# A sequential edge-removal pass beside four graph layers: the nearest removal handed over in SBUF instead of through DRAM

## The chip, the cores and the metric

The kernel runs on one core of one Trainium2 chip. The metric is the device time of one execution in microseconds (us). The time before is 6935.3 us, the median of three runs (6930.78 to 6940.25). One more execution was recorded by the hardware profiler; its span is 6932.5 us. The engines are named as in the profile: PE (matrix products), PEld (its weight loads), DVE (vector), ACT (scalar), POOL (GpSimd) and SP (SyncE, which here only issues DMAs).

## The reference, cut to what matters

Sixteen graphs of 1024 nodes with 128 features pass four layers with a residual and a layer norm after each. The first three (masked attention, a max over neighbours, a sum over neighbours with an MLP) use the adjacency as given. The fourth uses an adjacency from which edges have been removed first, row by row, each removal also changing later rows:

```python
def step(carry, n):
    row = carry[n]
    num = sum(row)
    sf = where(num > 10, (num + 1) // 2, 1)
    rank = cumsum(row)
    rm = row & (rank % sf == 0)          # only where the node counts and num > 1
    carry = carry.at[n].set(row & ~rm)
    carry = carry.at[:, n].set(carry[:, n] & ~rm)     # the symmetric column
    return carry
# for n = 0 .. 1023, in this order; then three rounds of
#   agg = (adj_d @ x) / deg;  out = normalised(agg @ Wr + x @ Wx + b);  h = batchnorm(relu(out))
```

The important point is the last line of the step: an edge removed in row n at position m must also be missing when row m is reached. A removal in one row has to be handed on, transposed, to all rows that come later.

## The kernel before

**Two stages.** `layers_012` computes the first three layers for one graph after another. The removal pass (`dilation`) depends only on the adjacency, so it runs beside them, for all 16 graphs at once. After that, the fourth layer runs alone (`edges`, `sage`, `convolve`).

**Slots.** The first stage is a loop over 1376 slots (86 for each of 16 graphs). In each half of a slot PE looks up a table (`look_up`, L769, into the PSUM tile `pg`, two buffers) and DVE takes a maximum of it (`best`, L821, 128x1024 elements). Everything else is put between these: generators yield the engine and cost of their next piece, and `advance` emits a piece where the planned room of its engine allows it. The instruction order of PE, ACT, DVE and POOL is the order in which this Python code emits them (`manual_schedule`). SP is not in that list: the order of the DMAs on its queue comes from the framework's scheduler. SP issues them one after another.

**Blocks of the removal pass.** The 1024 rows are cut into K = 32 blocks of R = 32 rows. A block of all 16 graphs lies on 128 partitions as 4 groups of 32 rows, with Q = 4 graphs side by side in the free dimension: `E` is [128, 4, 1024] of bytes. Two blocks go by for one graph of the slots, so that even blocks contain the start of a graph (`attend`, `scores` and the tables of the next graph begin there) and odd blocks don't. Block k runs through these steps, each due at a slot fixed by the numbers that `dilation` yields:

1. L578 and L579: edges that the block before removed are taken out of `E`; they come from SBUF as `next_T`. `spread` (L581) opens the block: it sums counts per row with a small matmul (L588).
2. 31 rows on POOL (L602 to L618). Each row is a chain of ten tiny POOL instructions on 16 partitions that decides what is removed inside the 32x32 square, and writes `hit`. One row follows from the one before.
3. Between the rows, one turn of `work` per row on DVE: first `remove` of block k-1 (`behind`), then `prepare` of block k+1.
4. `hit` goes to DRAM (L623) and comes back in another layout as `hit_p` (L626); DVE takes it out of `E` (L630 to L634) and works out each row's step and rank. The removal in the next block's columns is transposed at once into `next_T` (L668).

**`remove(k)`** ranks the edges of the whole row block (two scans, L553, per graph of a partition), marks the removed ones in `gone` (L559, two buffers), stores them to `removed` (L561, for the fourth layer), transposes those two and more blocks ahead into `last_T` (L564, one buffer, [128, 4, blocks after, 32]), and stores that to `removed_T` in DRAM (L565). It takes 16 turns.

**`prepare(k)`** builds `V`, the ranks inside the square, sends it through DRAM to 16 partitions (L521, L522), then reads everything that blocks 0 to k-2 removed from `removed_T` into `gone_T` (L526, one DMA for each q, one buffer), passes five empty turns, and takes it out of `E` (L533, one instruction for each q, the remaining edges summed into `counts[:, 0]`). ACT sums the columns to the right (L538).

The order of work around the change is thus: `removed_T` writes of block k-1 and `gone_T` reads for block k+1 both fall into the rows of block k, on the queue of SP, on which `hit`, `hit_p`, `above` and `V` stand too.

Of the kernel before, what the change touches and what calls it, by code (L numbers as in the profile page):

```python
# [29 lines left out]
F32 = mybir.dt.float32  # L30
F32R = mybir.dt.float32r
BF = mybir.dt.bfloat16
# [3 lines left out]
ALU = mybir.AluOpType  # L36
# [3 lines left out]
B, N, D, H2 = 16, 1024, 128, 256  # L40
P = 128
# [5 lines left out]
NP = -(-N // PS)  # L47
TG = 12
R, G = 32, 4
K, Q = N // R, B // G  # L50
# [21 lines left out]
def tile_graph_layers(ctx: ExitStack, tc, a, out):  # L72
    nc = tc.nc
# [93 lines left out]
    for b in range(B):  # L167
        q, g = divmod(b, G)
        nc.gpsimd.dma_start(out=half_rows[g * R:(g + 1) * R, :, q],
                            in_=a["nodemask"][b].rearrange("(k r) -> r k", r=R))  # L170
    nc.vector.tensor_scalar(half_rows, half_rows, 0.5, None, op0=ALU.mult)

    of_graph = consts.tile([P, G], F32, name="of_graph")
# [17 lines left out]
    removed_T = dram.tile([K, P, Q, N], BF, name="removed_T")  # L191
# [44 lines left out]
    def layers_012():  # L236
# [6 lines left out]
        dil = right.enter_context(tc.tile_pool(name="dil", bufs=1, side="right"))  # L243
# [237 lines left out]
        def dilation():  # L481
            adj_q = adj.rearrange("(q g) n m -> g n q m", g=G)
            axis = mybir.AxisListType.X
            hit = dil.tile([B, R, R], BF, name="hit")
            nc.gpsimd.memset(hit, 0.0)

            def load(k):
                own = slice(k * R, (k + 1) * R)
                E = dil.tile([P, Q, N], U8, name="E", bufs=3)
                for g in range(G):  # L490
                    nc.gpsimd.dma_start(out=E[g * R:(g + 1) * R], in_=adj_q[g, own])


                counts = dil.tile([P, 5, Q], F32, name="counts", bufs=2)
                nc.gpsimd.memset(counts, 0.0)
                V = dil.tile([B, R, R], BF, name="V", bufs=2)
                return E, V, counts

            def prepare(k, E, V, counts):
                own = slice(k * R, (k + 1) * R)  # L500
                square = dil.tile([P, Q, R], BF, name="square")
                nc.vector.tensor_copy(square, E[:, :, own])
                square_T = dil.tile([P, Q, R], BF, name="square_T")
                nc.vector.transpose(square_T.rearrange("p q m -> p (q m)"), square.rearrange("p q m -> p (q m)"))
                upper = dil.tile([P, Q, R], BF, name="upper")
                nc.vector.tensor_mul(upper, square, above)
                nc.vector.tensor_reduce(counts[:, 3, :], square, axis=axis, op=ALU.add)
                yield 1.3
                U = dil.tile([P, Q, R], BF, name="U")
                nc.vector.tensor_tensor_scan(U.rearrange("p q m -> p (q m)"), running.rearrange("p q m -> p (q m)"),  # L510
                                             upper.rearrange("p q m -> p (q m)"), 0.0, op0=ALU.mult, op1=ALU.add)
                nc.vector.tensor_copy(counts[:, 4, :], U[:, :, R - 1])
                nc.vector.tensor_sub(counts[:, 3, :], counts[:, 3, :], counts[:, 4, :])
                nc.vector.tensor_mul(upper, upper, square_T)
                far = dil.tile([P, Q, R], F32, name="far")
                nc.vector.scalar_tensor_tensor(far, U, FAR, upper, op0=ALU.add, op1=ALU.mult)
                Vp = dil.tile([P, Q, R], BF, name="Vp")
                nc.vector.tensor_scalar(Vp, far, -1.0, FAR, op0=ALU.mult, op1=ALU.add)
                Vd = dram.tile([B, R, R], BF, name=f"above{k}")
                for g in range(G):  # L520
                    nc.sync.dma_start(out=Vd.rearrange("(q g) n m -> g n q m", g=G)[g], in_=Vp[g * R:(g + 1) * R])  # L521
                nc.sync.dma_start(out=V, in_=Vd)  # L522
                if k > 1:
                    gone_T = dil.tile([P, Q, N], BF, name="gone_T")
                    for q in range(Q):
                        nc.sync.dma_start(out=gone_T[:, q, :(k - 1) * R],  # L526
                                          in_=removed_T[k, :, q, :(k - 1) * R])
                yield 2.0
                for _ in range(5):
                    yield 0  # L530
                for q in range(Q):
                    if k > 1:
                        nc.vector.scalar_tensor_tensor(  # L533
                            E[:, q, :(k - 1) * R], E[:, q, :(k - 1) * R], 1.0, gone_T[:, q, :(k - 1) * R],
                            op0=ALU.mult, op1=ALU.is_gt, accum_out=counts[:, 0, q:q + 1])
                    if k < K - 1:
                        junk = dil.tile([P, N], U8, name="junk")
                        nc.scalar.activation(junk[:, :N - (k + 1) * R], E[:, q, (k + 1) * R:], AF.Copy,  # L538
                                             accum_out=counts[:, 1, q:q + 1])
                    yield 0.6  # L540

            def remove(k, E, centre, scale, width):

                own = slice(k * R, (k + 1) * R)
                after = K - 2 - k
                if after > 0:
                    last_T = dil.tile([P, Q, after, R], BF, name="last_T")
                ranks = [None] * Q
                for q in range(Q + 1):
                    if q < Q:  # L550
                        rank = ranks[q] = dil.tile([P, N], F32, name="rank", bufs=2)
                        for h, s in enumerate(halves):
                            nc.vector.tensor_tensor_scan(rank[:, s], E[:, q, s], E[:, q, s],  # L553
                                                         rank[:, 511:512] if h else 0.0, op0=ALU.add, op1=ALU.max)
                            yield 1.3
                        nc.scalar.activation(rank, rank, AF.Abs, bias=centre[:, q:q + 1], scale=scale[:, q:q + 1])
                    if q:
                        gone = dil.tile([P, N], BF, name="gone", bufs=2)
                        nc.vector.scalar_tensor_tensor(gone, ranks[q - 1], width[:, q - 1:q], E[:, q - 1, :],  # L559
                                                       op0=ALU.is_equal, op1=ALU.mult)  # L560
                        nc.sync.dma_start(out=removed[k, :, q - 1, :], in_=gone)  # L561
                        yield 1.3
                        if after > 0:
                            nc.vector.transpose(last_T[:, q - 1].rearrange("p k r -> p (k r)"), gone[:, (k + 2) * R:])  # L564
                            nc.sync.dma_start(out=removed_T[k + 2:, :, q - 1, own].rearrange("k p r -> p k r"),  # L565
                                              in_=last_T[:, q - 1])
                            yield 0.8

            this, next_T = load(0), None
# [1 line left out]
                pass  # L571
            behind = iter(())
            for k in range(K):
                E, V, counts = this
                own = slice(k * R, (k + 1) * R)
                if k:
                    prev = slice((k - 1) * R, k * R)
                    nc.vector.tensor_tensor(E[:, :, prev], E[:, :, prev], next_T, op=ALU.is_gt)  # L578
                    nc.vector.tensor_reduce(counts[:, 2, :], E[:, :, prev], axis=axis, op=ALU.add)  # L579
                spread = dil.tile([P, 5, Q, G], F32, name="spread")  # L580
                nc.vector.tensor_mul(spread, counts.unsqueeze(3).to_broadcast([P, 5, Q, G]),  # L581
                                     of_graph.unsqueeze(1).unsqueeze(1).to_broadcast([P, 5, Q, G]))
                yield 0, 0.9, True
                p = shared("pc")
                own_bank = hold()
                for c, slots in enumerate(((0, 2, 3), (1, 4))):
                    for i in slots:
                        nc.tensor.matmul(p[:B, c * R:(c + 1) * R], spread[:, i].rearrange("p q g -> p (q g)"), of_row,  # L588
                                         start=(i == slots[0]), stop=(i == slots[-1]))
# [6 lines left out]
                work = [behind]  # L596
# [3 lines left out]
                work = (cost for part in work for cost in part)  # L600
                gp = nc.gpsimd
                for n in range(R - 1):  # L602
# [12 lines left out]
                    gp.tensor_scalar(last[:, n + 1:], V[:, n, n + 1:], to, None, op0=ALU.is_le)  # L615
                    gp.tensor_add(hit[:, n, n + 1:], hit[:, n, n + 1:], last[:, n + 1:])
                    gp.tensor_sub(low[:, n + 1:], low[:, n + 1:], hit[:, n, n + 1:])
                    yield 1.05, next(work, 0), False  # L618
                for cost in work:
                    yield 0.5, cost, False  # L620

# [3 lines left out]
                for g in range(G):  # L625
                    nc.sync.dma_start(out=hit_p[g * R:(g + 1) * R],  # L626
                                      in_=hit_d.rearrange("(q g) n m -> g n q m", g=G)[g])
                yield (B * NP - 10) / K - 34.55, 0, False
                hit_T = dil.tile([P, Q, R], BF, name="hit_T")
                nc.vector.transpose(hit_T.rearrange("p q m -> p (q m)"), hit_p.rearrange("p q m -> p (q m)"))  # L630
                nc.vector.tensor_tensor(E[:, :, own], E[:, :, own], hit_T, op=ALU.is_gt)
                nc.vector.tensor_reduce(counts[:, 3, :], E[:, :, own], axis=axis, op=ALU.add)
                num = dil.tile([P, Q], F32, name="num")
                nc.vector.tensor_reduce(num, counts[:, 0:4, :].rearrange("p s q -> p q s"), axis=axis, op=ALU.add)  # L634
                yield 0.5, 1.2, False

                half = dil.tile([P, Q], F32, name="half")
                nc.vector.scalar_tensor_tensor(half, num, 0.5, half_rows[:, k, :], op0=ALU.add, op1=ALU.mult)
# [521 lines left out]
```

## Time and profile before

| stretch of the span, us | length | PE busy | DVE busy | ACT busy | POOL busy |
|---|---|---|---|---|---|
| 0 to 136.2: weights, first graph's scores | 136.2 | 77.3 | 33.0 | 48.4 | 28.6 |
| 136.2 to 5560: slots with the removal pass | 5423.8 | 4511.4 | 4652.2 | 3149.4 | 3549.1 |
| 5560 to 6932.5: fourth layer | 1372.5 | 1100.0 | 616.4 | 538.8 | 262.7 |

The first bound of the second stretch is the first `spread` (L581), the last one lies after the last block's `hit_T` (L630). Busy time alone doesn't say what an engine is worth: an engine at 86% may be the one that all others wait for, and its idle time may have one cause or many. The views used below are: the 40 slices of the page; the groups of instructions by line, which give after the second bar the idle time of the engine just before them and what ended it; the waits (who waited for whom, total, times, longest); the time-line of one engine; and busy time by stretch. An "SPq" line is an issue or a wait of SP's queue. The granted clock of PE was 0.887 of full speed over the span.

### The profile page before, as it was taken

To read this page: it belongs to the slowest core of one execution; us is meant where nothing else is said; L and a number is where in the kernel's file an instruction comes from. 1 tells how busy PE (TensorE), PEld (TensorE's weight loads), DVE (VectorE), ACT (ScalarE), POOL (GpSimd) and SP (SyncE) were. 2 spreads that over 40 slices of the span, in tenths; PEclk is the share of its full clock that TensorE was granted. 3 is DMA by queue.
4 is the path that set the end of the run, shared out by engine and by line. 5 is a ranking of instruction groups with operands and counts; after the bars stand their busy time and mean duration, and the time that the engine had idled before them with its cause. 6 is when DMAs were issued, how large, how long until landed. Compare 5 with 4: busy or idle time off the path is not lost. (4 is left out here: it accounts for less than half of the span.)

```text
span 6932.5 us, 85659 instructions
## 1 busy us (share of the span) xinstructions
PE 5688.7 (82%) x27113; PEld 2882.3 (42%) x27242; DVE 5301.6 (76%) x8046; ACT 3736.6 (54%) x6537; POOL 3840.5 (55%) x11285
## 2 busy tenths in 40 slices
PE   6869898989697878888887878787897868787996
PEld 3424344444343434343443434343443335555653
DVE  3979899999797888888887979797898944444453
ACT  4646566666465555555565656565565523333851
POOL 3655767776657575757575757575777611110116
PEclk8979898999798989898988888888898878888998
DMA  5111212121212121212121212121211046554644
GB/s 36 16 21 21 32 24 33 20 32 19 32 20 26 25 27 24 27 24 27 24 29 22 30 21 30 21 30 21 32 20 23 14 74 115 112 112 110 215 140 158
DMA packets 494380, 318.97 MB, mean 46 GB/s; under 512 B 316650, under 2 KB 445668, under 8 KB 489828
## 3 DMA queue, kind: packets, MB, share of 16 engines
q0 software_dynamic: 105648, 84.20, 13.9%
q1 hardware_dynamic: 383600, 228.10, 11.4%
q8 instruction: 213, 3.49, 0.2%
q10 hardware_dynamic: 4676, 1.19, 0.1%
q14 instruction: 243, 1.99, 0.1%
HBM read 413.70 MB, written 118.16 MB: 77 GB/s over the span
## 5 line engine op out<-in xcount | busy, mean ns | idle before, releaser
L821 DVE TENSOR_TENSOR best<-best,pg 128x1024 f32<-128x1024 f32 x2720 | 3230.1, 1210 | 307.9 <-PE pg L769 298.9
L739 ACT ACTIVATE hot<-pm,one_less 128x512 fp32r<-128x512 f32 x2752 | 1884.9, 689 | 1257.8 <-PE pm L738 1246.9
L769 PE MATMUL pg<-hot,high 64*128 64x512 f32 x5504 | 1476.9, 533 | 763.3 <-DVE best L821 694.9
L769 PEld LDWEIGHTS pg<-hot,high 64*128 64x128 f32 x5504 | 546.8, 195 | 1569.5 <-DVE best L821 1076.6
L769 PE MATMUL pg<-hot,low 64*128 64x512 f32 x5504 | 1170.7, 422 | 0.0
L738 PE MATMUL pm<-AT,lit 120*128 120x512 fp8e4 x2752 | 1139.4, 414 | 7.9 <-ACT low L760 1.6
L607 POOL TENSOR_SCALAR sc<-low_counts,half_mask,rest 16x1 f32<-16x1 f32 x992 | 433.0, 436 | 397.6 <-DVE rest L594 304.1
L769 PEld LDWEIGHTS pg<-hot,low 64*128 64x128 f32 x5504 | 571.8, 204 | 0.0
L738 PEld LDWEIGHTS <-lit 120*128 120x128 fp8e4 x2752 | 274.2, 100 | 621.8 <-issue 558.1
L760 ACT CAST low<-pt 128x256 fp32r<-128x256 f32 x688 | 256.0, 372 | 473.6 <-PE pt L758 469.5
L612 POOL TENSOR_SCALAR sc<-sc 16x1 f32<-16x1 f32 x992 | 426.8, 430 | 105.1
L609 POOL TENSOR_SCALAR sc<-sc 16x1 f32<-16x1 f32 x992 | 351.6, 354 | 107.7
L970 POOL TENSOR_TENSOR length<-length,mhalf 128x8 f32<-128x8 f32 x48 | 78.9, 1644 | 571.7 <-DVE length L969 571.7
L615 POOL TENSOR_SCALAR last_rank<-V,sc 16x31 f32<-16x31 bf16 (+30 forms) x992 | 377.2, 380 | 0.0
L614 POOL TENSOR_SCALAR hit<-V,sc 16x31 bf16<-16x31 bf16 (+30 forms) x992 | 375.7, 379 | 0.0
L758 PE MATMUL pt<-high,less 128*128 128x256 f32 x688 | 300.5, 437 | 67.4 <-ACT high L753 60.7
L533 DVE SCALAR_TENSOR_TENSOR E<-E,gone_T 128x32 uint8<-128x32 uint8 (+29 forms) x120 | 80.2, 669 | 325.4 <-DMA gone_T<-removed_T 325.4
L467 DVE TENSOR_TENSOR sub<-sub,q 128x24 f32<-128x24 f32 (+11 forms) x768 | 304.8, 398 | 24.7 <-ACT q L289 10.5
L750 PE MATMUL pt<-ident,sub 128*128 128x128 f32 x1376 | 293.7, 298 | 34.7 <-ACT hot L739 32.1
L610 POOL TENSOR_SCALAR sc<-sc 16x1 f32<-16x1 f32 x992 | 272.4, 275 | 83.3
L927 ACT CAST m<-near 128x1024 fp32r<-128x1024 fp8e4 x256 | 253.4, 1045 | 112.9 <-DVE near L896 59.9
L377 PE MATMUL pav<-v,eT 128*128 128x128 f32 x2048 | 307.3, 296 | 2.0 <-ACT eT L370 2.0
(255 smaller groups left out, 9614.6 us busy)
## 6 DMA issues: line engine op xcount, KB each, us to landing
removed<-gone SPq DMA_DIRECT2D x128, 256.0 KB
An<-in_adj_dram POOLq DMA_DIRECT2D x16, 1024.0 KB, 15.7
E<-in_adj_dram POOLq DMA_DIRECT2D x128, 128.0 KB, 6.7
gone_all<-removed POOLq DMA_DIRECT2D x64, 256.0 KB, 12.0
near<-in_adjT_dram POOLq DMA_DIRECT2D x16, 1024.0 KB, 17.4
h<-x SPq DMA_DIRECT2D x32, 512.0 KB
kept<-near SPq DMA_DIRECT2D x16, 1024.0 KB
share<-share SPq DMA_DIRECT2D x32, 512.0 KB
```

What stands on the lines that cost most here:

```text
L377: nc.tensor.matmul(pav, eT[:, c, :], values[b][:, c, :], start=(c == 0), stop=(c == T - 1))
L467: nc.vector.tensor_max(sub[:, :n_g, n:2 * n], sub[:, :n_g, 0:n], qg[:, 2 * g0:2 * g0 + n_g, k:k + 1].to_broadcast([P, n_g, n]))
L607: gp.tensor_scalar(half, mine, half_mask[:, m], rest[:, n:n + 1], op0=ALU.mult, op1=ALU.add)
L609: gp.tensor_scalar(sf, half, 5.5, sf, op0=ALU.is_gt, op1=ALU.mult)
L612: gp.tensor_scalar(to, at, sf, none, op0=ALU.subtract, op1=ALU.subtract)
L614: gp.tensor_scalar(hit[:, n, n + 1:], V[:, n, n + 1:], at, None, op0=ALU.is_equal)
L615: gp.tensor_scalar(last[:, n + 1:], V[:, n, n + 1:], to, None, op0=ALU.is_le)
L738: nc.tensor.matmul(pm, lit[:, r, :], AT[b * (T + 1) + c][:, halves[h]], start=True, stop=True)
L739: nc.scalar.activation(hots[s][:, halves[h]], pm, AF.Relu, bias=one_less)
L758: nc.tensor.matmul(pt, less, high, start=False, stop=True, skip_group_check=True)
L769: nc.tensor.matmul(pg[:, a], part[rows, at * P:(at + 1) * P], hots[s][rows, halves[h]], start=(k == 0), stop=(k == 1))
L821: nc.vector.tensor_max(own, own, pg)
```

## The change

What block k+1 needs of the removal in block k-1 is already in SBUF when it is prepared: it is the first of the blocks in `last_T`. The change takes it from there, with a comparison and a sum of its own and a sixth slot in `counts`. Only what blocks 0 to k-2 removed then comes through DRAM, and that was written a block earlier; so the read of `gone_T` is moved from the middle of the rows to `load`, which is called ahead of the first row. It is meant to take the trip through DRAM out of the rows in which the removal is made. The five empty turns, which had given that trip time, go, and the rows become due every 1.03 slots instead of 1.05 with the pause after them adjusted, so that a block has the same number of slots.

```diff
+            last_T = None
             def load(k):
...
+                gone_T = None
+                if k > 2:
+                    gone_T = dil.tile([P, Q, N], BF, name="gone_T")
+                    for q in range(Q):
+                        nc.sync.dma_start(out=gone_T[:, q, :(k - 2) * R],
+                                          in_=removed_T[k, :, q, :(k - 2) * R])
...
-                counts = dil.tile([P, 5, Q], F32, name="counts", bufs=2)
+                counts = dil.tile([P, 6, Q], F32, name="counts", bufs=2)
...
-            def prepare(k, E, V, counts):
+            def prepare(k, E, V, gone_T, counts):
...
                 nc.sync.dma_start(out=V, in_=Vd)
+                yield 2.0
                 if k > 1:
-                    gone_T = dil.tile([P, Q, N], BF, name="gone_T")
-                    for q in range(Q):
-                        nc.sync.dma_start(out=gone_T[:, q, :(k - 1) * R],
-                                          in_=removed_T[k, :, q, :(k - 1) * R])
-                yield 2.0
-                for _ in range(5):
-                    yield 0
+                    at = slice((k - 2) * R, (k - 1) * R)
+                    nc.vector.tensor_tensor(E[:, :, at], E[:, :, at], last_T[:, :, 0, :], op=ALU.is_gt)
+                    nc.vector.tensor_reduce(counts[:, 5, :], E[:, :, at], axis=axis, op=ALU.add)
+                    yield 0.6
                 for q in range(Q):
-                    if k > 1:
+                    if k > 2:
                         nc.vector.scalar_tensor_tensor(
-                            E[:, q, :(k - 1) * R], E[:, q, :(k - 1) * R], 1.0, gone_T[:, q, :(k - 1) * R],
+                            E[:, q, :(k - 2) * R], E[:, q, :(k - 2) * R], 1.0, gone_T[:, q, :(k - 2) * R],
                             op0=ALU.mult, op1=ALU.is_gt, accum_out=counts[:, 0, q:q + 1])
...
             def remove(k, E, centre, scale, width):
+                nonlocal last_T
...
                             nc.vector.transpose(last_T[:, q - 1].rearrange("p k r -> p (k r)"), gone[:, (k + 2) * R:])
-                            nc.sync.dma_start(out=removed_T[k + 2:, :, q - 1, own].rearrange("k p r -> p k r"),
-                                              in_=last_T[:, q - 1])
+                            if after > 1:
+                                nc.sync.dma_start(out=removed_T[k + 3:, :, q - 1, own].rearrange("k p r -> p k r"),
+                                                  in_=last_T[:, q - 1, 1:])
...
-                spread = dil.tile([P, 5, Q, G], F32, name="spread")
+                spread = dil.tile([P, 6, Q, G], F32, name="spread")
...
-                for c, slots in enumerate(((0, 2, 3), (1, 4))):
+                for c, slots in enumerate(((0, 2, 3, 5), (1, 4))):
...
-                    yield 1.05, next(work, 0), False
+                    yield 1.03, next(work, 0), False
...
-                yield (B * NP - 10) / K - 34.55, 0, False
+                yield (B * NP - 10) / K - 33.93, 0, False
...
                 nc.vector.tensor_reduce(num, counts[:, 0:4, :].rearrange("p s q -> p q s"), axis=axis, op=ALU.add)
-                yield 0.5, 1.2, False
+                nc.vector.tensor_add(num, num, counts[:, 5, :])
+                yield 0.5, 1.3, False
```

More of the change, by code (lines that the diff above doesn't have):

```diff
@@ L491, in load @@
                     nc.gpsimd.dma_start(out=E[g * R:(g + 1) * R], in_=adj_q[g, own])
-                counts = dil.tile([P, 5, Q], F32, name="counts", bufs=2)
+                gone_T = None
[5 more added lines that the diff above has]
+                counts = dil.tile([P, 6, Q], F32, name="counts", bufs=2)
                 nc.gpsimd.memset(counts, 0.0)
                 V = dil.tile([B, R, R], BF, name="V", bufs=2)
-                return E, V, counts
-            def prepare(k, E, V, counts):
+                return E, V, gone_T, counts
+            def prepare(k, E, V, gone_T, counts):
                 own = slice(k * R, (k + 1) * R)
@@ L573, in dilation @@
             for k in range(K):
-                E, V, counts = this
+                E, V, _, counts = this
                 own = slice(k * R, (k + 1) * R)
@@ L579, in dilation @@
                     nc.vector.tensor_reduce(counts[:, 2, :], E[:, :, prev], axis=axis, op=ALU.add)
-                spread = dil.tile([P, 5, Q, G], F32, name="spread")
-                nc.vector.tensor_mul(spread, counts.unsqueeze(3).to_broadcast([P, 5, Q, G]),
-                                     of_graph.unsqueeze(1).unsqueeze(1).to_broadcast([P, 5, Q, G]))
+                spread = dil.tile([P, 6, Q, G], F32, name="spread")
+                nc.vector.tensor_mul(spread, counts.unsqueeze(3).to_broadcast([P, 6, Q, G]),
+                                     of_graph.unsqueeze(1).unsqueeze(1).to_broadcast([P, 6, Q, G]))
                 yield 0, 0.9, True
```

## The prediction

> **What bounds the kernel now.** I read the 40 slices first: DVE is at 8 or 9 tenths until slice 32, about 5560 us, and at 4 or 5 after it, so there are two stages, and the change lies in the first. There DVE is busy 4652.2 of 5423.8 us (the table of stretches, 136.2 to 5560). PE is busy 4511.4 us but waits for DVE at L769 694.9 us. DVE's instructions run in one written order, so I then asked what ends DVE's idle time. The groups by line (busy us, mean ns, then idle before and its releaser):
>
> ```profile
> L821 DVE TENSOR_TENSOR best<-best,pg 128x1024 f32<-128x1024 f32 x2720 | 3230.1, 1210 | 307.9 <-PE pg L769 298.9
> L533 DVE SCALAR_TENSOR_TENSOR E<-E,gone_T 128x32 uint8<-128x32 uint8 (+29 forms) x120 | 80.2, 669 | 325.4 <-DMA gone_T<-removed_T 325.4
> ```
>
> L821 does most of the work and waits in crumbs; L533 works for 80 us and holds DVE idle for 325. The waits of DVE, 136.2 to 5423 us (total, times, longest), give the sizes:
>
> ```profile
> DVE E L533 <- DMA gone_T<-removed_T: 325.4, 15, 43.3
> DVE best L821 <- PE pg L769: 297.0, 532, 10.4
> DVE hit_T L630 <- DMA hit_p<-hit: 49.3, 11, 10.7
> ```
>
> Split by shape, L533 waits before ten widths only: 32 (43.3 us), then 320, 384, 448, 512, 576, 640, 704, 768 and 832 (35.8, 37.5, 34.6, 27.7, 29.7, 29.5, 29.6, 29.6, 28.0). A width of 32(k-1) is block k being prepared inside block k-1, so these are block 1 and the even blocks 10 to 26. I cut the trace at L581, which opens a block. Columns: stretch, its us, busy us of PE, PEld, DVE, ACT, POOL with counts, clock, DMA share, GB/s. Blocks 8, 14, 15 and 28:
>
> ```profile
> 1443.70:1608.90 165.20, 146.29 (x734) 73.74 (x739) 149.80 (x223) 107.36 (x193) 112.01 (x333) 0.95 0.24 27
> 2473.50:2670.70 197.20, 148.32 (x726) 74.59 (x730) 151.47 (x229) 106.12 (x192) 113.15 (x332) 0.84 0.18 22
> 2670.70:2824.50 153.80, 133.71 (x663) 61.83 (x665) 140.91 (x206) 93.24 (x176) 111.02 (x342) 0.95 0.18 29
> 4927.90:5094.00 166.10, 144.33 (x699) 70.85 (x701) 151.68 (x226) 102.01 (x186) 115.58 (x330) 0.90 0.17 24
> ```
>
> Blocks 8 and 28 carry block 14's DVE work (149.8 and 151.7 against 151.5 us) and have no such wait; they are 32 and 31 us shorter. Block 15 is an odd block, lighter, also without it. Why block 14 waits is in the time-line of SyncE's queue, then of DVE:
>
> ```profile
> 2529.66 0.32 SPq L561 DMA_DIRECT2D removed<-gone  x1
> 2604.94 0.33 SPq L623 DMA_DIRECT2D hit<-hit  x1
> 2605.37 0.37 SPq L565 DMA_DIRECT2D removed_T<-last_T  x1
> ...
> 2608.47 0.34 SPq L526 DMA_DIRECT2D gone_T<-removed_T  x1
> ```
> ```profile
> 2610.82 0.62 DVE L533 SCALAR_TENSOR_TENSOR E<-E,gone_T 128x448 uint8<-128x448 uint8 x1 [33.11 <-DMA gone_T<-removed_T]
> ```
>
> In this block the queue holds `hit<-hit` (L623) ahead of two of the `removed_T` writes and of the `gone_T` reads behind them. `hit` is ready only when POOL's 31 rows are done, so the queue stood still for 75 us:
>
> ```profile
> SPq L623 <- POOL low_counts L617: 75.1, 1, 75.1
> ```
>
> In block 8 the same queue issues `hit<-hit` last, and nothing waits. DVE's wait is thus a place in a queue, not bandwidth: DMA engines are at 0.06 share while it lasts.
>
> **What the Trainium skill says.** "DMA: Bandwidth & Descriptors", "Anatomy of one DMA — SWDGE (gpsimd) path" (the sentence is on all of them): DMA engines do not wait on semaphores; the issuing sequencer does, before dispatch. The 75.1 us agree: what stands behind the waiting issue isn't issued either. "SBUF — State Buffer", "Who interferes with whom": VectorE and GpSimd share a port pair, locked for a whole instruction. The trace agrees: one POOL row (L607 to L607) took 4.25 us at 2539.69 beside a busy DVE and 3.15 us at 2599.02 while DVE stood. "TensorE: Matmul & The Clock Gate", Part 1: an idle window of about 3.4 us halves PE's clock. The trace agrees: 0.59 granted in the stalled 2577.6 to 2610.8, 0.88 in the 29 us after, 1.00 in the next 31.
>
> **The change, part by part.**
> 1. *The read of `gone_T` moves to the load of a block, at the first row, and stops at the block three back.* What it needs was written by the removal that ran a whole block earlier; its late writes went out at about 136 us of a block (2609.8 in block 14), some 30 us before the shortened block ends. The first row meets them landed, and L533 comes some 70 us later. So the 325.4 us should go. What is it worth? The nine stalled even blocks sum to 1773.8 us; at block 28's 166.1 they would be 1494.9: -279. Block 1 is 184.0 us with 43.3 of wait and 135.7 of DVE work; at a DVE share of 92% (151.7 of 166.1) it would be 147: -37, or -43 if all the wait goes. I take -39, so **-318**. That is 98% of the wait: PE and ACT run ahead only by the two `pg` buffers, and PE's half clock after a stall goes too.
> 2. *The nearest removal from SBUF.* Per block DVE gets one comparison like L578 (0.28 us), one sum like L579 (0.29), one addition of 128x4 in `num` (L634's 0.18), and 16 more elements in L581, whose 80 take 0.24 (0.02): 0.77. Off come 32 elements in each of four L533: the shapes go from 186 ns at 32 to 1150 at 960, 33 ns each, 0.13. Net 0.64 x 30 = 19 us. Block 2 loses its four small L533 and their accumulator reads (4 x 0.27, less the 0.13 already counted): -1. DVE is busy for 91% of the stage without the waits (4530 of 5287 less 325), so of 18 us I put **+16** on the path; ends 9 and 18, as half or all of it is on it.
> 3. *One more matmul in L588*, 0.23 us a block, 7 us in all: hidden, since PE waits 695 us for DVE.
> 4. *One `removed_T` slab fewer, four SP waits of some 3 us for a write's landing (353.9 us in total at L526) gone*: the queue's own time, behind which only `above`, `V` and `hit` stand; nothing on the path. *`counts` larger*: a 0.12 us memset, on POOL ahead of the rows, nothing.
> 5. *Five empty turns out of the preparation, rows due every 1.03 slots, the pause adjusted*: a block still has the same slots (32.55 + X - 34.55 = 31.93 + X - 33.93). L533 comes five rows earlier; by part 1 its data is long there. Nothing.
> 6. *New waits.* The reads of `gone_T` wait on SP for the last L533, done in the block before. DVE's comparison reads `last_T`, written by DVE itself three turns earlier. Behind a `gone_T` read on SP stand `removed` and `removed_T`, which DVE needs only through `gone` (two buffers) and `last_T`.
>
> Sum: 6935.3 - 318 + 16 = **6633 us**; without recovery effects (-325 to -310) and the ends of part 2 it runs from 6619 to 6643.
>
> **The rivals.**
> - *The rows become the wait.* Without idle DVE time POOL gets no fast rows. For: odd blocks already wait at L630 (49.3 us in all). Against: block 8, without a stall, had its last row at 1572.3, the last `hit_p` issue at 1578.0, and DVE at L630 only at 1599.3, 19 us after it could have landed. In block 14 eight or nine fast rows turn slow, +9 us, and DVE arrives at 153 us of the block instead of 187; hit would be there at about 145. If 5 to 10 us were lost in each of nine blocks: 6680 to 6725.
> - *The queue stalls somebody else.* SP's order is not written out by hand, and may change. If `hit<-hit` slips ahead of the second `removed` write, the fourth `gone` (L559) has no buffer and DVE stops at about 63 us of the block (the fourth `gone` starts at 2536.4 in block 14) until the rows end: (63-3)/4.2 = 14 rows done, 17 x 3.15 = 54, some 55 us with the write. In the ten blocks: 6935 - 318 + 16 + 550 = **7183, slower**. For: in blocks 10 and 12 it already stands directly behind that quarter. Against: nothing ahead of that point on DVE changes, and the place would have to move by 16 us of the block. In two blocks alone: 6743.
> - *PE takes over.* If only half of the wait is saved, 6790. Against: after block 14's stall DVE waited for PE 0.2 to 1.2 us a time, under a recovering clock; blocks 8 and 28 run without the stall and PE isn't their limit.
> - *Nothing*: would need L533's wait to be hidden; the pairs 8/14 and 28/14 say it isn't.
>
> **How the numbers follow.** Chances: forecast 0.80, rows 0.08, queue 0.06 (a third of it in a few blocks only), PE 0.05, nothing 0.01. The time is the forecast's, 6633. The range is 6600 to 6710: below, a stronger gain from the clock and from less queueing on SP; above, most of the rows case. Left out are PE, the queue, and tails of the forecast. Faster 0.93, same 0.02, slower 0.05.
>
> **What would show it.** Right: L533's idle under 10 us; even blocks 10 to 26 at about 167 us, odd ones at 154; PE's clock in them near 0.93; waits of L630 below 100 us; the second stage unchanged at 1372 us. Part 2 shows as two new DVE groups of 30 with 0.28 to 0.29 us. Wrong: a new long wait on DVE at `gone`, `last_T` or `hit_T` with a DMA as releaser, or PE's `pg` waits growing by over 100 us.

## The result and the profile after

The changed kernel takes 6613.1 us (median of four runs, 6611.3 to 6616.1) against 6933.6 us for the kernel before, run beside it: a ratio of 0.9537, 95% interval 0.952 to 0.9553, which is 320 us less. The forecast was 6633 us. The second stage is as it was, about 1372 us; the whole gain lies in the stage of the slots.

The groups of DVE by line, in the changed kernel (busy us, mean ns, idle before and its releaser). L540 is the old L533; L535 and L536 are new:

```profile
L831 DVE TENSOR_TENSOR best<-best,pg 128x1024 f32<-128x1024 f32 x2720 | 3234.4, 1210 | 309.0 <-PE pg L779 300.5
L540 DVE SCALAR_TENSOR_TENSOR E<-E,gone_T 128x32 uint8<-128x32 uint8 (+28 forms) x116 | 75.3, 649 | 0.0
L536 DVE TENSOR_REDUCE counts<-E 128x4 f32<-128x128 uint8 x30 | 8.6, 286 | 1.0
L535 DVE TENSOR_TENSOR E<-E,last_T 128x128 uint8<-128x128 uint8 x30 | 8.4, 281 | 0.0
```

325.4 us of idle time ahead of one line have become 0.0, and the two new groups cost 17 us in 30 blocks. The waits of DVE from the first block to the last (137 to 5104 us):

```profile
DVE best L831 <- PE pg L779: 295.6, 560, 6.7
DVE hit_T L639 <- DMA hit_p<-hit: 43.2, 8, 9.7
```

Nothing has taken the place of the wait: both lines are within 7 us of before. The same four blocks as in the prediction, 8, 14, 15 and 28 (length, then busy us of PE, PEld, DVE, ACT, POOL, then clock, DMA share, GB/s):

```profile
1402.20:1566.10 163.90, 147.23 (x750) 73.48 (x746) 151.82 (x228) 108.16 (x194) 111.27 (x333) 0.95 0.25 27
2356.00:2522.10 166.10, 149.33 (x734) 74.70 (x732) 151.79 (x232) 106.07 (x192) 113.64 (x332) 0.90 0.21 26
2522.10:2676.60 154.50, 136.00 (x667) 62.79 (x667) 141.25 (x209) 93.57 (x176) 111.08 (x342) 0.93 0.18 29
4604.80:4772.30 167.50, 143.83 (x707) 70.34 (x703) 152.48 (x229) 101.92 (x186) 115.58 (x330) 0.92 0.17 24
```

Block 14 went from 197.2 to 166.1 us, with the same DVE work; the others moved by 1.4 us at most. Cut at L590 (which opens a block now), the nine even blocks 10 to 26 sum to 1483.9 us against 1773.8, block 1 is 149.3 against 184.0, and the other 21 blocks together are 5 us longer.

One thing did not change: the standstill of SP's queue. Its time-line in block 14 (2356.0 to 2522.1), and its longest wait there:

```profile
2413.65 0.32 SPq L569 DMA_DIRECT2D removed<-gone  x1
2488.04 0.33 SPq L632 DMA_DIRECT2D hit<-hit  x1
...
2490.52 0.39 SPq L574 DMA_DIRECT2D removed_T<-last_T  x1
...
2499.02 1.80 SPq L498 DMA_DIRECT2D gone_T<-removed_T  x4
```
```profile
SPq L632 <- POOL low_counts L626: 74.2, 1, 74.2
```

`hit` still holds the queue for 74 us ahead of two `removed_T` writes. DVE no longer asks in these rows for anything behind it. The last line also shows where the reads of `gone_T` really are: not at the first row, but in the block before, and still behind `hit`. A read at the end of block 14 is for block 16; it goes out when its data has landed, L540, which in block 14 works for block 15, has freed the buffer, and `hit` has gone. It is L540 in block 15 that uses it, from 2598.7 us on, 100 us later. (In odd blocks from 5 on, where `hit` stands last, the reads go out at 87 to 92 us of the block; in the even blocks 8 to 28 at 138 to 145.)

### The profile page after: what moved, and what is told of

Same layout as the page of the kernel before. It is cut to its first block, busy times and chain, and to the rows that moved or that the text cites. A ratio compares the mean times of both kernels' runs of the same rounds, so it can differ in the third digit from the quotient of the medians.

```text
span 6611.5 us, 85916 instructions
## 1 busy us (share of the span) xinstructions
PE 5697.7 (86%) x27306; PEld 2883.8 (44%) x27306; DVE 5317.7 (80%) x8130; ACT 3733.9 (56%) x6537; POOL 3844.7 (58%) x11285
## 5 line engine op out<-in xcount | busy, mean ns | idle before, releaser
L621 POOL TENSOR_SCALAR sc<-sc 16x1 f32<-16x1 f32 x992 | 430.1, 434 | 105.0
L618 POOL TENSOR_SCALAR sc<-sc 16x1 f32<-16x1 f32 x992 | 341.8, 345 | 107.7
L619 POOL TENSOR_SCALAR sc<-sc 16x1 f32<-16x1 f32 x992 | 270.1, 272 | 83.3
L617 POOL TENSOR_SCALAR sc<-sc 16x1 f32<-16x1 f32 x992 | 256.6, 259 | 86.6
```

What stands on the lines that cost most here:

```text
L618: gp.tensor_scalar(sf, half, 5.5, sf, op0=ALU.is_gt, op1=ALU.mult)
L621: gp.tensor_scalar(to, at, sf, none, op0=ALU.subtract, op1=ALU.subtract)
```

## The experiments

The theory: DVE waited for a place in SP's queue, behind `hit`; what the change did was to let nothing that DVE needs in these rows stand there. Rivals: the trip through DRAM was too long in itself; the early issue or the smaller read is what helped; the pace of the rows helped.

**1. Only the place, on the kernel before.** The DMAs of `hit` leave SP for POOL, which has just computed it; all else is as before, trip through DRAM, empty turns and pace included.

```diff
-                nc.sync.dma_start(out=hit_d, in_=hit)
+                nc.gpsimd.dma_start(out=hit_d, in_=hit)
...
-                    nc.sync.dma_start(out=hit_p[g * R:(g + 1) * R],
+                    nc.gpsimd.dma_start(out=hit_p[g * R:(g + 1) * R],
```

> The kernel before, with the five DMAs of hit (L623, L626) issued from POOL instead of SP; nothing else. SP's queue then holds removed, removed_T, gone_T, above and V only, in the order of the work. Theory (the wait of L533 is a place in SP's queue behind hit, not the trip through DRAM): L533's idle time falls from 325 us to under 15, and the time to 6935 - 318 = about 6617 us, with the DRAM trip, the five empty turns and the row pace all as before. Rival 1 (the trip removed_T to gone_T is itself too long for the rows): at least half of the idle time stays, 6780 us or more. Rival 2 (only the handover in SBUF helps): 6935 us. If POOL's own wait for the landing of hit costs, some 5 us in each of 32 blocks, at most 6770 us with the wait named at POOL.

Measured: 6568.7 us, ratio 0.947 (0.9456 to 0.9484). The group of L533 and SP's queue near the end of a block's removal:

```profile
L533 DVE SCALAR_TENSOR_TENSOR E<-E,gone_T 128x32 uint8<-128x32 uint8 (+29 forms) x120 | 80.3, 669 | 0.0
```
```profile
2397.99 0.37 SPq L565 DMA_DIRECT2D removed_T<-last_T  x1
2401.10 0.32 SPq L526 DMA_DIRECT2D gone_T<-removed_T  x1
2405.66 1.74 SPq L521 DMA_DIRECT2D above<-Vp  x4
```

The idle time at L533 is gone without any handover in SBUF: from the issue of a `removed_T` write to that of the read behind it pass 3 us, and DVE has no wait left there. Both rivals named in the expectation fall. The cost feared for POOL is there, 57.6 us of waits, but they come after the rows, and the time is lower all the same:

```profile
POOL hit_p L626 <- DMA hit<-hit: 57.6, 32, 3.2
```

But the kernel is 48 us faster than the theory said, and 44 us faster than the changed kernel; experiments 2 and 7 are about that.

**2. The same on the changed kernel**, the same two edits.

> The changed kernel with the five DMAs of hit issued from POOL instead of SP. Theory: the changed kernel has no DVE wait left that comes from hit's place in the queue, so 6613 us within 12; DVE's waits for hit_p (54 us) may move by 20. Rival (SP's standstill still costs, through above, V or gone): 6560 to 6595 us.

Measured: 6580.7 us, ratio 0.9487 (0.9472 to 0.9501). This is 32 us below the changed kernel, outside the 12 us that my theory allowed, and the rival's number holds. Its reason was left open by this run. Against experiment 1 the run prices the change on a queue without the standstill: the whole change then costs 12 us (6580.7 - 6568.7; the runs lie at 6575.6 to 6583.0 and 6565.3 to 6570.6) and gains nothing.

**3. The read written back among the rows**, handover kept.

```diff
             def load(k):
...
-                        nc.sync.dma_start(out=gone_T[:, q, :(k - 2) * R],
-                                          in_=removed_T[k, :, q, :(k - 2) * R])
...
             def prepare(k, E, V, gone_T, counts):
...
                 nc.sync.dma_start(out=V, in_=Vd)
+                        nc.sync.dma_start(out=gone_T[:, q, :(k - 2) * R],
+                                          in_=removed_T[k, :, q, :(k - 2) * R])
```

> The changed kernel with the read of gone_T written back where it stood, among the rows in prepare, still stopping at the block three back. Theory: what counts is what the read depends on, not where it is written; its data has landed a block earlier, and SP's order, which the scheduler makes from dependencies, has the reads in the same places as in the changed kernel. 6613 us within 12, no idle time at the line of gone_T. Rival (the early issue at the first row is what helps): the reads stand behind hit again, 6850 to 6940 us.

Measured: 6611.3 us, ratio 0.9531 (0.9515 to 0.9547), no idle time before the line of `gone_T`. The reads stand in SP's queue where they stood: in block 14 last, from 144 us of the block on (143 in the changed kernel). So the written place makes no difference; and since the issue did not move, this run doesn't test what the early issue is worth. That neither an early issue nor a smaller read is needed is shown by experiment 1, which has neither.

**4. The nearest 32 columns through DRAM again**, the rest early.

```diff
-                            if after > 1:
-                                nc.sync.dma_start(out=removed_T[k + 3:, :, q - 1, own].rearrange("k p r -> p k r"),
-                                                  in_=last_T[:, q - 1, 1:])
+                            nc.sync.dma_start(out=removed_T[k + 2:, :, q - 1, own].rearrange("k p r -> p k r"),
+                                              in_=last_T[:, q - 1])
...
+                    for q in range(Q):
+                        nc.sync.dma_start(out=piece[:, q, :], in_=removed_T[k, :, q, at])
...
-                    nc.vector.tensor_tensor(E[:, :, at], E[:, :, at], last_T[:, :, 0, :], op=ALU.is_gt)
+                    nc.vector.tensor_tensor(E[:, :, at], E[:, :, at], piece, op=ALU.is_gt)
```

> The changed kernel, but the 32 columns of the nearest removal go through DRAM again (written with removed_T, read in prepare as four small reads of 64 bytes a partition), the rest of gone_T read early as in the change. Theory (the place behind hit): in block 1 and the even blocks 8 to 26 these reads stand behind hit, and DVE asks for them at about 78 us of the block, earlier than L533 did at 104; it stops until the rows end, about 42 us of fast rows and 6 us of DMA: 11 x 48 = 530 us more, about 7140 us, slower than the kernel before although far less is read. Rival (the amount to be read late is what costs): 13 times less data, so 6640 us at most.

Measured: 7261.0 us, ratio 1.0468 (1.0453 to 1.0484): slower than the kernel before. The line that reads the small piece, and SP's queue in an even block:

```profile
L539 DVE TENSOR_TENSOR E<-E,piece 128x128 uint8<-128x128 uint8 x30 | 8.7, 288 | 641.3 <-DMA piece<-removed_T 578.9 <-issue 62.4
```
```profile
2744.64 0.33 SPq L635 DMA_DIRECT2D hit<-hit  x1
...
2750.21 0.34 SPq L536 DMA_DIRECT2D piece<-removed_T  x1
...
2754.55 0.32 SPq L536 DMA_DIRECT2D piece<-removed_T  x1
```

Eleven waits, 641 us, for reads of 64 bytes a partition: a small read doesn't help behind `hit`. The mechanism and the number of blocks were right; each wait was 58 us instead of the 48 I worked out. In these eleven blocks DVE asked at 79 us of the block on average and the rows ended at 129: 50 us, where I had put 42 for rows that run fast while DVE stands, and the DMAs after them took 9 us, not 6. The run also shows which half of the change carries it: with the early read but without the handover it loses.

**5. The old pace of the rows**, with four empty turns so that L540 comes at the turn it had before.

```diff
+                for _ in range(4):
+                    yield 0
...
-                    yield 1.03, next(work, 0), False
+                    yield 1.05, next(work, 0), False
...
-                yield (B * NP - 10) / K - 33.93, 0, False
+                yield (B * NP - 10) / K - 34.55, 0, False
```

> The changed kernel with the row pace of before: rows due every 1.05 slots, the pause 34.55, and four empty turns ahead of the gone_T comparison, so that it comes at the same turn as before. Theory (pace and turns hide nothing, part 5 of the prediction): 6613 us within 8. Rival (part of the 320 us is from the new pace): 6625 to 6700 us.

Measured: 6611.7 us, ratio 0.9531 (0.9518 to 0.9544). The pace is worth nothing that shows: the runs of both kernels lie between 6608 and 6616 us.

**6. The new sum five times**, to price DVE work in these rows (the added line stands four times).

```diff
                     nc.vector.tensor_reduce(counts[:, 5, :], E[:, :, at], axis=axis, op=ALU.add)
+                    nc.vector.tensor_reduce(counts[:, 5, :], E[:, :, at], axis=axis, op=ALU.add)
```

> The changed kernel with the new sum of 128x128 into counts (0.29 us of DVE) made five times instead of once: 4 x 0.29 x 30 = 35 us more DVE work, its result unchanged. It prices the term that the prediction put at 91% on the path (+16 us for 18 us of work). At 91%: 6613 + 32 = 6645 us. Theory now, from the 20 blocks that had no stall before and have none after (they grew by 5 us for about 10 us of added work): a half, 6613 + 17 = 6630 us. Rival (DVE has room): 6613 us.

Measured: 6635.7 us, ratio 0.9564 (0.9551 to 0.9577): 22.5 us for 34.3 us of work (4 x 30 sums of 286 ns), two thirds, between the two expectations. The interval is some 9 us to each side, so the share is not sharp, and the 91% of the prediction is not excluded; experiment 2 against 1 points the same way, 12 us for the 16 that the change adds to DVE's busy time.

**7. Where the extra 32 us are.** In the odd blocks 5 to 27 of the changed kernel the rows end at 133 us on average, and in half of these blocks DVE waits at L639. The time-line of block 15 just after the rows, SP, POOL and DVE:

```profile
2654.55 0.33 SPq L632 DMA_DIRECT2D hit<-hit  x1
2655.75 2.21 POOL L493 DMA_DIRECT2D E<-in_adj_dram  x4
2656.14 2.55 SPq L635 DMA_DIRECT2D hit_p<-hit  x4
...
2666.51 0.31 DVE L639 STREAM_TRANSPOSE hit_T<-hit_p 128x128 bf16<-128x128 bf16 x1 [5.75 <-DMA hit_p<-hit]
```

POOL, free at last, issues the 512 KB of the next `E` in the very moment in which the 32 KB of `hit_p` are on the way. To test it, the loads of `E` are put behind an instruction that waits for DVE; `hit` stays on SP:

```diff
             def load(k):
-                for g in range(G):
-                    nc.gpsimd.dma_start(out=E[g * R:(g + 1) * R], in_=adj_q[g, own])
...
                 nc.gpsimd.memset(counts, 0.0)
+                for g in range(G):
+                    nc.gpsimd.dma_start(out=E[g * R:(g + 1) * R], in_=adj_q[g, own])
```

> The changed kernel, in load the memset of counts set ahead of the four loads of E on POOL instead of behind them; hit stays on SP. The memset waits for L666 of the block (start_at), so the loads of E no longer start when the rows end, while hit_p is on its way, but some 10 us later. It asks why hit on POOL gave 32 us beyond the changed kernel. Theory (the 512 KB of E, issued at 134 us of an odd block, share the DMA engines with hit_p, issued at 134.6 to 136.1, and DVE then waits at L639): the time from the last hit_p issue to L639 in the odd blocks falls from about 9 us to 5, the 54 us of waits at L639 by half or more, and the time to 6580 to 6592 us. Rival 1 (SP's own issue, or its queue standing still in even blocks, is what costs): no change, 6613 us within 8. Rival 2 (the rows start later, as POOL issues E between the blocks): slower, 6620 to 6680 us.

Measured: 6588.7 us, ratio 0.9501 (0.9488 to 0.9514). The group of L639, of the changed kernel and of this one:

```profile
L639 DVE STREAM_TRANSPOSE hit_T<-hit_p 128x128 bf16<-128x128 bf16 x32 | 9.8, 307 | 54.3 <-DMA hit_p<-hit 54.2
```
```profile
L639 DVE STREAM_TRANSPOSE hit_T<-hit_p 128x128 bf16<-128x128 bf16 x32 | 9.8, 306 | 30.8 <-DMA hit_p<-hit 30.8
```

The waits fall by 23 us, a little less than the half that I expected; nearly all that is left stands in blocks 1, 3 and 31. The time falls by 24. The waits alone are a rough measure (experiments 3 and 5 have 62.8 and 70.9 us there at the changed kernel's time), but the blocks agree: the odd ones from 5 to 27 fell from 155.2 to 152.8 us on average. From the last `hit_p` issue to L639 they took 9.0 us on average in the changed kernel and take 6.3 here. So the collision explains 24 of the 32 us; by what means the loads delay `hit_p` no run shows. With `hit` on POOL its place in that queue puts `hit_p` ahead of `E` (from 135.5 and from 138.2 us of block 15 in experiment 2), which has the same effect on the order. The remaining 8 us are about what the intervals leave open, and I don't assign them.

**The fastest version** is that of experiment 1, 6568.7 us: the kernel before with five DMAs of each block on another queue, ratio 0.947 against 0.9537 for the change.

## Why the prediction was right, point by point

- *The bound and its cause* (`hit<-hit` ahead of the reads on SP, 75 us of standstill): shown by experiments 1 and 4, from both sides. (The 40 slices were misread in a detail: DVE is at 7 to 9 tenths there, not 8 or 9.)
- *Part 1, -318 us*: right. The even blocks fell by 289.9 us (forecast 279) and block 1 by 34.7 (39), 324.6 in all, although each already carries its share of the new work. For block 1 the sum had a slip: 151.7 of 166.1 is 91%, not 92%, which makes its forecast 149 us instead of 147, and 149.3 was measured. The even blocks last 164.9 us on average, forecast 167; PE's half clock after the stall is gone from them (0.84 to 0.90 in block 14).
- *"The first row meets them landed"*: wrong in detail. The reads are issued in the block before, and in the even blocks 8 to 28 behind `hit`; experiment 3 shows that their written place is worth nothing. The time was right because they are a block ahead of their use: in block 14 the standstill still delays them, but 100 us are left.
- *Part 2, +16 us*: the work was sized well: DVE's busy time from the first block to the last rose by 16.1 us (4529.8 to 4545.9; forecast 18). The share on the path, 91%, was probably too high. Experiments 6 and 2 give two thirds and three quarters, and the 21 blocks without a stall grew by 5 us for about 11 us of new work (20 of its 30 shares). All three lie below 91%, none is sharp. The weak step took DVE's busy share of the stage for the share of an added microsecond that shows. In the odd blocks the path to L639 often runs through POOL's rows and `hit_p`, not through DVE: with five sums DVE reaches the 73rd maximum of these blocks (5 to 27) 1.8 us later than in the changed kernel, but the blocks are only 1.0 us longer on average. The slots' stage fell by 320 us where parts 1 and 2 give 302. Of these 18 us, 12 lie in the ten stalled blocks (-324.6, against -318 and their third of the 16) and 6 in the others (+5, against 11).
- *Part 3 to 5, nothing*: the extra matmul, the smaller queue and the pace; experiment 5 shows it for the pace. *Part 6*: no new wait appeared.
- *The rows become the wait*: did not happen in the even blocks 10 to 26, where on average the last `hit_p` is issued at 135.1 us and L639 comes at 154.4. The 9 us of slower rows did not come either: the rows of these blocks end at 131.9 us, against 131.2 before. For them the prediction compared two rows of block 14 and put the difference down to DVE, but the row of 4.25 us has a piece of other work on POOL behind its ten instructions:

```profile
2539.69 0.33 POOL L607 TENSOR_SCALAR sc<-low_counts,half_mask,rest 16x1 f32<-16x1 f32 x1
...
2543.21 0.68 POOL L690 DMA_DIRECT2D AT<-in_adjT_dram  x1 [0.29 <-issue]
2543.94 0.32 POOL L607 TENSOR_SCALAR sc<-low_counts,half_mask,rest 16x1 f32<-16x1 f32 x1
```

The next two rows took 3.39 and 3.42 us, with DVE at work. And the row that took 3.15 us during the stall takes 3.15 us in block 14 of the changed kernel too (2482.11 to 2485.26), where DVE is busy for 23.6 of the 27.2 us from 2461.0 to 2488.2. So these two rows don't show the shared port pair that the prediction cites for them, and the standstill had not made the rows of this block fast; the last section has what other rows show. As a floor of the odd blocks it was there before and is there after; I had seen its 49 us and not asked what made `hit_p` slow.

- *The queue stalls somebody else*: did not happen, and the order stayed about where it was: `hit` stands ahead of the third `removed` write in blocks 8 and 10 (before: 10 and 12), never ahead of the second, on which the fourth `gone` waits. Experiment 4 shows what such a place costs. (The working of this rival put 4.2 us to a row. In the even blocks 10 to 26 the eleventh row ended at 60 us and the twelfth at 65, so at 63 us 11 rows would have been done, not 14.)

## What to carry to other kernels

When an engine waits for a DMA, read the time-line of the queue that issues it before you shorten the transfer: here the answer was one issue, waiting for a slow chain, ahead of others that were ready. Here the DMAs that wait for the long chain were best issued by the engine that ends the chain: what stands behind them there, the loads of `E`, can wait. And price added work by an experiment, or by which wait ends last in each kind of block, not by the busy share of a stage.

## What the hardware showed that I had not expected

Small transfers came late beside a large one. In block 15 of the changed kernel DVE was released 7.8 us after the last of four `hit_p` issues of 8 KB had ended (2658.7 to 2666.5), with 512 KB for `E` in flight; issued from POOL ahead of `E`, in experiment 1, one such DMA took 1.9 us from issue to landing (median). With the loads of `E` put later, in experiment 7, DVE's waits at L639 in the odd blocks 5 to 27 went from 25.9 us in all to 1.1.

A busy DVE does not slow POOL's rows as such; it depends on the instruction that a row meets. In the trace of the kernel before, L612, one of the ten, took 0.37 us on average both where it overlapped `best` alone (578 times) and where DVE was idle (103 times), but 1.07 us where it overlapped a scan of `rank` (L553, 31 times). Why is not shown here. Nor does a standstill of DVE win much for the rows: in experiment 4, with 49 to 66 us of it in each of the even blocks 10 to 26, the rows ended at 129.0 us on average, against 131.9 in the changed kernel.
